# Earlier loads, spread stores and edge transposes on VectorE in a graph-network kernel

## The chip, the cores and the metric

The kernel runs on one core of one Trainium2 chip. The metric is the device time of one execution in microseconds (us). The kernel before takes 17,993.09 us, the median of three runs (17,978.58 to 18,013.7).

## The reference

There are 50,000 nodes with a row x of 160 numbers each (64 scalars and 32 vectors of 3), and 1,650,000 directed edges (src, dst), sorted by dst, with four numbers `edge_attr_4` each. Every node also has one edge to itself among them. Cut to what matters:

```python
ss, vv = s[src], v[src]                       # gather the source's row
out0 = C0 * (ss * e0 @ W1 + dot * INV3 @ W2)  # linear in x[src], and in the edge's four numbers
...
m_agg = jax.ops.segment_sum(m, dst, num_segments=n)
hs = m_agg[:, :MUL0] @ Ws * LIN_S
hv = jnp.einsum('nui,uw->nwi', m_agg[:, MUL0:].reshape(n, MUL1, 3), Wv) * LIN_V
x = _layernorm(x + (x + jax.nn.relu(h)))
```

A message is linear in x[src] and in the edge's four numbers. So for each node it is enough to sum four weighted copies of the gathered rows (one for each number k) and to multiply the sums by one combined matrix afterwards. The kernel does that.

## The kernel before

**Units, groups, pairs, stages.** A unit is 128 edges. A group is G = 6 units (768 edges); the kernel has 2087 groups and 12,522 units. A pair is two groups (12 units), 1044 in all; a stage is 20 groups, that is ten pairs, 105 stages. The program is written out in full, in one long loop over the pairs (the loop at the end of the function, `for p, (s, g, ng) in enumerate(pairs)`).

**One pair.** `gather` (L344 on) issues 12 indirect DMAs on POOL (L349), each of which fetches 128 rows of x into a slice of the tile `xg`; the pool of `xg` has four buffers, so the gathers of a pair wait until TensorE has read those of four pairs earlier. `spread` (L353 on) makes on VectorE a one-hot tile `hot` (L358) that says which of 32 node slots an edge belongs to, and `ha` (L361), the one-hot times each of the four edge numbers. `group_sums` (L386) multiplies on TensorE: `ha` of a unit stands as the weights, the gathered rows are the moving data, and six units add up in PSUM. `turn_sums` transposes the result in 32x32 blocks on VectorE (L398) and adds it (L405) at a place known only at run time to `ring`, a tile that holds the sums of a segment of 512 nodes (four blocks of 128). When a new segment begins, the tail of the old ring is added to the head of the new one (L402).

**One stage.** `load` asks on the SP queue for the indices and numbers of the next stage (L257 from the list `edges`, or L263 to L265 from the inputs for the first five stages), at the stage's first pair. `place`, four pairs later, brings them from one unit on a partition to one edge of each unit on a partition: TensorE transposes source and target indices (L326, L327) and the four numbers (L331) into PSUM, and a matmul with ones (L320) spreads the first node of each group, taken out by VectorE (L318), to all partitions; VectorE then makes `baseB` (L322), the integer indices `si` (L334) for the gathers, and `rel` (L337). In TensorE's queue these matmuls stand between those of L386, and TensorE runs its queue in order.

**Packs.** A node's edge to itself needs no gather. For all but the first 100 groups these edges are taken out: a pack is 128 rows of 790 edges. `read` fetches them on SP (L474 to L478, a tile of one buffer); ScalarE and VectorE mark the edges to themselves, move the others together by log-steps of predicated copies (L566), sum the four numbers of the ones taken out, and `store` writes each row by a DMA of its own to a place known at run time in `edges`, and its self-numbers to `selves` (L618, 16 DMAs a step after a read of registers, L601). There are 16 packs. A pack is a list of 77 steps, 17 of them stores, which are dealt out evenly between the end of the last pack and the pack's due pair.

**Blocks.** When a block of 128 nodes is complete, `block` multiplies its columns of the ring by the combined weights (L704), VectorE adds the node's own rows `xt` (asked for by L644 at the pair at which the block's last group runs) and norms them (L182 to L196), ScalarE takes the root (L191), SP writes two blocks (L784). For the edges to themselves, `ask_own` (six pairs before the segment) fetches 256 rows of x four times, once to each 32 partitions, in one DMA (`xr`, L675), and one number for each row (`sr`, L676: 1024 pieces of four bytes); `set_own` (two pairs before) multiplies them on VectorE (L689) and transposes them into the new ring (L693), which they start.

**What orders the work.** On SP, TensorE, VectorE and ScalarE the instructions run in the order in which the program writes them; `after_pair(p, f)` puts a task in a list that is handed over when pair p is written, and `work(1.0)` writes one unit of such tasks after each of the 12 units of a pair. SP's queue holds all loads and stores, and a DMA that must wait for its data (L784 for VectorE's `o`) holds those behind it.

Of the kernel before, what the change touches and what calls it, by code (L numbers as in the profile page):

```python
# [50 lines left out]
P = 128  # L51
MUL0, MUL1 = 64, 32
D = MUL0 + 3 * MUL1
NK = 4
# [21 lines left out]
KM = 31  # L76

# [25 lines left out]
def tile_gnn_resnorm(ctx: ExitStack, tc: tile.TileContext, x, src, dst, attr, W1, W2, W3, W4, W5, Ws, Wv, out, n_edges):  # L103
# [123 lines left out]
    with tc.tile_pool(name="once", bufs=1) as once, tc.tile_pool(name="raw", bufs=2) as rawp, \  # L227
# [17 lines left out]
        nc.vector.tensor_copy(slotsP, slots)  # L245

# [3 lines left out]
        def load(s):  # L250

            g0 = s * SG
            n = (min(NG, g0 + SG) - g0) * G
            if g0 >= NH:
                p0 = g0 * G * P - EH
                r6 = rawp.tile([P, P, 2 + NK], F32, name="r6")
                dq.dma_start(r6[:n].rearrange("u p c -> u (p c)"),  # L257
                             edges[0, p0 * (2 + NK):(p0 + n * P) * (2 + NK)].rearrange("(u q) -> u q", u=n))
                return s, n, None, r6[:n, :, 0], r6[:n, :, 1], r6[:n, :, 2:]
            e = slice(g0 * G * P, (g0 * G + n) * P)  # L260
            ri = rawp.tile([P, 2, P], I32, name="ri")
            ra = rawp.tile([P, P, NK], F32, name="ra")
            dq.dma_start(ri[:n, 0, :], src1[e].rearrange("(u p) o -> u (p o)", p=P))  # L263
            dq.dma_start(ri[:n, 1, :], dst1[e].rearrange("(u p) o -> u (p o)", p=P))
            dq.dma_start(ra[:n].rearrange("u p k -> u (p k)"), attr[e].rearrange("(u p) k -> u (p k)", p=P))  # L265
            return s, n, ri, None, None, ra[:n]

        def cast(loaded):
            s, n, ri, sf, df, af = loaded
            if ri is not None:  # L270
                rf = rawp.tile([P, 2, P], F32, name="rf")
                begun.append(nc.scalar.copy(rf[:n], ri[:n]))
                sf, df = rf[:n, 0, :], rf[:n, 1, :]
            return s, n, sf, df, af
# [37 lines left out]
        def place(cast_):  # L312

            s, n, sf, df, af = cast_
            ng = n // G

            first = idxp.tile([P, SG], F32, name="first")
            nc.vector.tensor_scalar(first[:n], starts[:n], df[:, 0:1], None, op0=ALU.mult)  # L318
            yield 1
            nc.tensor.matmul(bank[:, 3, :ng], ones[:n], first[:n, :ng], start=True, stop=True)  # L320
            baseB = idxp.tile([P, SG], F32, name="baseB")
            nc.vector.tensor_scalar(baseB[:, :ng], bank[:, 3, :ng], float(N - 1), None, op0=ALU.min)  # L322
            aim(s, ng, baseB)
            yield 1
            pi = bank[:, 1:3, :]
            nc.tensor.transpose(pi[:, 0, :n], sf, ident[:n, :n])  # L326
            nc.tensor.transpose(pi[:, 1, :n], df, ident[:n, :n])  # L327
            yield 1.5
            pk = psK.tile([P, NK, P], F32, name="pk")
            for k in range(NK):  # L330
                begun.append(nc.tensor.transpose(pk[:, k, :n], af[:, :, k], ident[:n, :n]))  # L331
                yield 0.75
            si = idxp.tile([P, P], I32, name="si")
            nc.vector.tensor_scalar(si[:, :n], pi[:, 0, :n], 0.0, float(N - 1), op0=ALU.max, op1=ALU.min)  # L334
# [3 lines left out]
                rel[:, :n].rearrange("p (g j) -> p g j", j=G), pi[:, 1, :n].rearrange("p (g j) -> p g j", j=G),  # L338
                float(N - 1), baseB[:, :ng].unsqueeze(2).to_broadcast([P, ng, G]),
# [3 lines left out]
            placed[s] = si, rel, pk  # L343
# [50 lines left out]
        def turn_sums(p, ps):  # L394
# [4 lines left out]
            for i in range(ng):  # L399
                k = seg_of[g + i]  # L400
                if k and g + i == first_of[k]:
                    nc.vector.tensor_tensor(ring[k][:, :, :TW - S], ring[k][:, :, :TW - S], ring[k - 1][:, :, S:],  # L402
                                            op=ALU.add)
# [337 lines left out]
        def after_pair(p, f, *args):  # L741
            later.setdefault(p, []).append((f, args))
# [313 lines left out]
```

## Time and profile before

| what | value |
|---|---|
| median of three runs | 17,993.09 us |
| time of the profiled execution | 18,022.17 us |
| its span | 18,020.0 us |
| busy: POOL, VectorE, TensorE matmul, ScalarE | 12,137.8, 7,032.6, 6,879.0, 227.8 us |
| DMA engines' mean share | 24% on POOL's queue, 6% on SP's |
| granted TensorE clock | 0.625 |

The profile's page has the busy time of each engine, the span in 40 slices, DMA queues, the chain that ended last, and groups of instructions with what ended the idle time before them. Asked further, the trace gives waits by engine and line, and the instructions of a stretch in order of time. "Issue" is idle time that ends with nothing that the trace shows; "remote" is a semaphore that something outside the traced instructions raised, or one that the trace could not assign.

### The profile page before, as it was taken

How to read it: one execution, taken by the hardware profiler on the slowest of the kernel's cores; microseconds unless marked ns; L12 is line 12 of the kernel's file. 1: busy time of each engine (PE TensorE's matmuls, PEld its weight loads, DVE VectorE, ACT ScalarE, POOL GpSimd, SP SyncE). 2: the span in 40 equal slices, each digit the busy share in tenths (PEclk: the TensorE clock that was granted, in tenths of full speed). 3: DMA queues.
4: the chain of work that ended last, by engine and by line, in shares of the span. 5: the costliest groups of instructions: out<-in, count | busy, mean ns of one | idle time of the engine just before them, and what ended most of it. 6: DMA issues, size and time to landing. Idle time of an engine off the chain costs nothing. (4 is left out here: it accounts for less than half of the span.)

```text
span 18020.0 us, 99721 instructions
## 1 busy us (share of the span) xinstructions
PE 6879.0 (38%) x29811; PEld 6014.7 (33%) x29812; DVE 7032.6 (39%) x11269; ACT 227.8 (1%) x479; POOL 12137.8 (67%) x12535
## 2 busy tenths in 40 slices
PE   3333334343333333333333333334333333333333
PEld 3333333333333333333333333333333333333333
DVE  4343443434434343443433434344343433434332
ACT  0000000000000000000000000000000000000000
POOL 6666666666666666666666666666666666666666
PEclk6666666666666666666666666666666666666666
DMA  2222323232232322323223232322323223232222
GB/s 71 74 69 72 80 71 81 69 82 72 73 79 70 83 71 73 79 69 81 72 72 79 70 79 72 82 69 72 80 70 82 69 73 80 69 79 72 73 72 63
DMA packets 961715, 1337.18 MB, mean 74 GB/s; under 512 B 411739, under 2 KB 716048, under 8 KB 957182
## 3 DMA queue, kind: packets, MB, share of 16 engines
q0 software_dynamic: 601056, 1026.60, 23.7%
q1 hardware_dynamic: 358674, 302.87, 6.1%
q8 instruction: 238, 3.90, 0.1%
q14 instruction: 307, 2.51, 0.0%
q10 hardware_dynamic: 1440, 1.29, 0.0%
HBM read 1258.50 MB, written 71.40 MB: 74 GB/s over the span
## 5 line engine op out<-in xcount | busy, mean ns | idle before, releaser
L349 POOL DMA_INDIRECT xg<-in_x,si x12522 | 12134.1, 969 | 5859.5 <-issue 3666.1
L386 PE MATMUL ps<-xg,ha 128*128 128x160 f32 x25044 | 6255.4, 383 | 9081.8 <-issue 8146.9
L386 PEld LDWEIGHTS ps<-xg,ha 128*128 128x128 f32 x25044 | 5171.1, 254 | 9859.0 <-issue 8902.6
L398 DVE STREAM_TRANSPOSE sums<-ps 128x320 f32<-128x320 f32 x1044 | 529.7, 507 | 6341.5 <-remote 4050.5
L361 DVE TENSOR_TENSOR ha<-hot,pk 128x1536 f32<-128x1536 f32 x1044 | 1830.2, 1753 | 35.8
L182 DVE SCALAR_TENSOR_TENSOR y<-phb,xt 128x160 f32<-128x160 f32 x391 | 125.6, 321 | 3508.3 <-PE ps L386 1623.2
L704 PE MATMUL phb<-BWk,ring 128*128 128x160 f32 (+1 forms) x3910 | 1181.7, 388 | 454.0 <-issue 452.9
L704 PEld LDWEIGHTS phb<-BWk,ring 128*128 128x128 f32 (+1 forms) x3910 | 925.6, 266 | 470.0 <-issue 469.5
L405 DVE TENSOR_TENSOR ring<-ring,sums 128x160 f32 x2087 | 683.1, 327 | 309.7 <-issue 224.2
L358 DVE TENSOR_TENSOR hot<-bank,rel 128x384 f32<-128x384 f32 x1044 | 572.4, 548 | 107.0 <-remote 70.5
L693 DVE STREAM_TRANSPOSE ring<-xr 128x1280 f32<-128x1280 f32 x188 | 466.1, 2479 | 6.5
L566 DVE COPY_PREDICATED prow<-marks,prow 128x2370 f32<-128x2370 int32 (+8 forms) x160 | 445.4, 2784 | 1.1
L320 PE MATMUL bank<-first,ones 120*128 120x20 f32 (+1 forms) x210 | 59.4, 365 | 815.1 <-DVE first L318 573.0
L320 PEld LDWEIGHTS bank<-first,ones 120*128 120x128 f32 (+1 forms) x210 | 49.8, 292 | 853.6 <-DVE first L318 597.5
L191 ACT ACTIVATE rstd<-mv,eps_t 128x1 f32<-128x1 f32 x391 | 115.2, 295 | 17061.4 <-DVE st L184 5415.1
L326 PE MATMUL bank<-ident,r 120*128 120x120 f32 x100 | 46.2, 462 | 703.1 <-issue 361.0
L566 DVE COPY_PREDICATED pra<-marks,pra 128x1580 f32<-128x1580 int32 (+8 forms) x160 | 306.5, 1915 | 0.0
L689 DVE TENSOR_TENSOR xr<-xr,sr 128x1280 f32<-128x1280 f32 x188 | 277.0, 1473 | 57.4 <-DMA sr<-selves 35.9
L326 PEld LDWEIGHTS bank<-ident,r 120*128 120x128 f32 x100 | 21.1, 211 | 727.4 <-issue 369.7
L196 DVE TENSOR_SCALAR o<-y,mv,rstd 128x160 f32<-128x160 f32 x391 | 146.1, 374 | 19.6 <-issue 3.7
L402 DVE TENSOR_TENSOR ring<-ring 128x1280 f32<-128x1280 f32 x97 | 143.0, 1474 | 1.8
L331 PE MATMUL pk<-ident,r 120*128 120x120 f32 (+1 forms) x400 | 139.5, 400 | 0.0
(349 smaller groups left out, 2156.2 us busy)
## 6 DMA issues: line engine op xcount, KB each, us to landing
xg<-in_x,si POOLq DMA_INDIRECT x12522
xr<-in_x SPq DMA_DIRECT2D x187, 640.0 KB
edges<-prow SPq DMA_DIRECT2D x1994, 18.5 KB
r<-edges SPq DMA_DIRECT2D x99, 360.0 KB
selves<-mine SPq DMA_DIRECT2D x1992, 0.5 KB
xt<-in_x SPq DMA_DIRECT2D x195, 160.0 KB
out<-o SPq DMA_DIRECT2D x195, 160.0 KB
pra<-in_attr SPq DMA_DIRECT2D x15, 1580.0 KB
```

Of the source, the lines that this page charges most:

```text
L196: nc.vector.tensor_scalar(o[:n], y[:n], mv[:n, 0:1], rstd[:n], op0=ALU.subtract, op1=ALU.mult)
L349: nc.gpsimd.indirect_dma_start(out=xg[:, j, :], out_offset=None, in_=x, in_offset=bass.IndirectOffsetOnAxis(ap=placed[0][:, u + j:u + j + ...
L358: nc.vector.tensor_tensor(hot[:, :n], slotsP[:, 0:W].unsqueeze(1).to_broadcast([P, n, W]), rel[:, u:u + n].unsqueeze(2).to_broadcast([P, n ...
L361: nc.vector.tensor_tensor(ha[:, :n], hot[:, :n].unsqueeze(2).to_broadcast([P, n, NK, W]), pk[:, :, u:u + n].rearrange("p k u -> p u k").un ...
L386: mm = nc.tensor.matmul(ps[:, j // G, :], ha[:, j].rearrange("p k w -> p (k w)"), xr, start=j % G == 0, stop=j % G == G - 1)
L398: nc.vector.transpose(at[:, :ng], ps[:, :ng].rearrange("p g (b f) -> p g b f", f=FB))
L402: nc.vector.tensor_tensor(ring[k][:, :, :TW - S], ring[k][:, :, :TW - S], ring[k - 1][:, :, S:], op=ALU.add)
L405: nc.vector.tensor_tensor(here, here, at[:, i], op=ALU.add)
L566: nc.vector.copy_predicated(what[:n, a:e], mi[:, r].unsqueeze(2).to_broadcast([n, e - a, what.shape[2]]), what[:n, a + d:e + d])
L689: nc.vector.tensor_tensor(xr[:, :nq], xr[:, :nq], sr[:, :nq].unsqueeze(2).to_broadcast([P, nq, D]), op=ALU.mult)
L693: nc.vector.transpose(ring[k][:, :, c0:c0 + nq * W].rearrange("p b (w q) -> p q b w", q=nq), xr[:, :nq].rearrange("p q (b f) -> p q b f", ...
L704: wrote("misc", nc.tensor.matmul(ph[:nb], ring[k][:, i, c0:c0 + nb], BWk[:, i, :], start=i == 0, stop=i == ND - 1))
```

## The change

1. **Loads.** `load` is asked for three pairs earlier (`LEAD = 3`), and it fetches in another layout: a partition gets four runs of 32 edges, one from each of four units. It always fetches 128 units. The first node of each group comes by a small DMA of its own (L269, `fi` or `fd`).
2. **Turning.** `place` uses VectorE's 32x32 transpose three times (L343, L349, L352) in place of the matmul with ones and the six transposes on TensorE.
3. **Packs.** The reading of the next pack (`follow`) stands in front of the last pack's stores; the stores come in every other step, and 15 empty steps follow. With these a pack is 105 steps (the first 109), and the due pair is earlier, by three pairs or two.
4. **Own rows.** `xr` comes in four DMAs (L700) in four successive pairs, from eight pairs before the segment; `selves` comes as it lies (`sa`, L705: 128 pieces of 128 bytes), and VectorE picks the number: `sa` times a mask in PSUM (L711), a sum (L712) into PSUM, and `xr` times that (L713).
5. **Rings.** The tail of the old ring is added in five instructions of some 133 to 166 columns (L425) in place of one of 1280.
6. **Node rows.** `xt` is asked for three pairs earlier.

The lines of the changed kernel are those of its own listing. Cut to its core:

```diff
+REST = 15
+LEAD = 3
+        shareP, sumP = bank[:, 3, 64:64 + NK], bank[:, 3, 96:96 + BP * P // W]
@@ load
-                r6 = rawp.tile([P, P, 2 + NK], F32, name="r6")
-                dq.dma_start(r6[:n].rearrange("u p c -> u (p c)"),
-                             edges[0, p0 * (2 + NK):(p0 + n * P) * (2 + NK)].rearrange("(u q) -> u q", u=n))
+            def fetch(to, what, c):
+                rows = what.rearrange("(u i q) -> i u q", u=P, i=NK)
+                dq.dma_start(to, rows)
+            def fetch_first(to, what, c):
+                firsts = what.rearrange("(g q) -> g q", g=W)[:, 0:1]
...
+                    dq.dma_start(to, firsts.unsqueeze(0).to_broadcast([NK, W, 1]))
...
+                r6 = rawp.tile([P, NK, W, C], F32, name="r6")
+                fd = rawp.tile([P, 1], F32, name="fd")
+                fetch_first(fd, edges[0, q0 * C + 1:(q0 + W * G * P) * C + 1], C)
+                fetch(r6.rearrange("p b e c -> p b (e c)"), edges[0, p0 * C:(p0 + P * P) * C], C)
@@ place
-            nc.vector.tensor_scalar(first[:n], starts[:n], df[:, 0:1], None, op0=ALU.mult)
-            yield 1
-            nc.tensor.matmul(bank[:, 3, :ng], ones[:n], first[:n, :ng], start=True, stop=True)
-            nc.vector.tensor_scalar(baseB[:, :ng], bank[:, 3, :ng], float(N - 1), None, op0=ALU.min)
+            nc.vector.transpose(baseB, fd.to_broadcast([P, W]))
+            base = baseB[:, f0:f0 + ng]
+            nc.vector.tensor_scalar(base, base, float(N - 1), None, op0=ALU.min)
...
-            nc.tensor.transpose(pi[:, 0, :n], sf, ident[:n, :n])
-            nc.tensor.transpose(pi[:, 1, :n], df, ident[:n, :n])
-            yield 1.5
+            nc.vector.transpose(pi.rearrange("p c (l b) -> p c b l", b=NK), ef)
+            yield 1
             pk = psK.tile([P, NK, P], F32, name="pk")
-            for k in range(NK):
-                begun.append(nc.tensor.transpose(pk[:, k, :n], af[:, :, k], ident[:n, :n]))
-                yield 0.75
+            begun.append(nc.vector.transpose(pk.rearrange("p k (l b) -> p k b l", b=NK), af.rearrange("p b e k -> p k b e")))
+            yield 1
@@ turn_sums
-                    nc.vector.tensor_tensor(ring[k][:, :, :TW - S], ring[k][:, :, :TW - S], ring[k - 1][:, :, S:],
-                                            op=ALU.add)
+                    past = max(high[first_of[k - 1]:first_of[k]]) + W - k * S
+                    for b in range(ND):
+                        nc.vector.tensor_tensor(ring[k][:, b, :past], ring[k][:, b, :past], ring[k - 1][:, b, S:S + past],
+                                                op=ALU.add)
@@ pack
-            steps += [read, None, None, None, begin]
+            steps.append(begin)
...
-            steps += [None, None]
-            steps += [None, None]
+            steps += [None, None, follow, None]
...
-                steps.append(partial(store, head, j))
-            return steps + [stored]
+                steps += [partial(store, head, j), None]
+            return read, steps + [stored] + [None] * REST
@@ set_own
-            xr, sr, nq = got
-            nc.vector.tensor_tensor(xr[:, :nq], xr[:, :nq], sr[:, :nq].unsqueeze(2).to_broadcast([P, nq, D]), op=ALU.mult)
+            xr, sa, nq = got
+            nc.vector.tensor_tensor(sa[:, :nq], sa[:, :nq], shareP.unsqueeze(1).to_broadcast([P, nq, NK]), op=ALU.mult)
+            nc.vector.tensor_reduce(sumP[:, :nq], sa[:, :nq], axis=AX.X, op=ALU.add)
+            nc.vector.tensor_tensor(xr[:, :nq], xr[:, :nq], sumP[:, :nq].unsqueeze(2).to_broadcast([P, nq, D]), op=ALU.mult)
@@ the plan and the loop over pairs
-            due.append(min((first - 1) * per - 1, first_of[own] // PG - 7))
-            packs.append(pack(i))
+            due.append(min((first - 1) * per - 1 - LEAD, first_of[own] // PG - 9))
+            packs.append(pack(i, lambda i=i: reads[i + 1]() if i + 1 < npacks else None))
+        packs[0][:0] = [reads[0], None, None, None]
...
-                after_pair(p - 6, ask_own, k, bs, got)
+                for part in range(NK):
+                    after_pair(p - 8 + part, ask_own, k, bs, got, part)
...
-            after_pair(max(p, START - 1), do_ahead, b)
+            after_pair(max(p - 3, START - 1), do_ahead, b)
...
+            if (p + LEAD) % per == 0 and (p + LEAD) // per + 1 < NSC or not p:
+                ahead_ = (p + LEAD) // per + 1
...
+                raws[ahead_] = load(ahead_)
             if p % per == 0 and s + 1 < NSC:
-                raws[s + 1] = load(s + 1)
```

## Prediction

> **What bounds the kernel now.** I read the page's busy shares and groups first, then POOL's waits, then stretches of the timeline.
>
> ```profile
> span 18020.0 us, 99721 instructions
> PE 6879.0 (38%) x29811; PEld 6014.7 (33%) x29812; DVE 7032.6 (39%) x11269; ACT 227.8 (1%) x479; POOL 12137.8 (67%) x12535
> ...
> L349 POOL DMA_INDIRECT xg<-in_x,si x12522 | 12134.1, 969 | 5859.5 <-issue 3666.1
> ```
>
> POOL's gathers fill the span. One takes 949 ns in the median (the tile view of xg), and 0.306 us lie behind each (3666.1 / 11991 below), so 12,522 of them need 15,715 us. What lies above that is of two kinds: long gathers, 12,134.1 - 12,522 x 0.949 = 251 us, and stands.
>
> ```profile
> POOL xg L349 <- issue: 3666.1, 11991, 2.1
> POOL xg L349 <- PE ps L386: 1224.7, 236, 46.9
> POOL xg L349 <- remote: 875.2, 223, 7.0
> POOL xg L349 <- PE phb L704: 64.3, 12, 6.7
> ```
>
> With two single waits of 5.9 and 5.6 the stands are 2,176 us in 473 pieces, 4.6 us each, nearly all ahead of a pair's first gather: xg has four buffers, and TensorE has not yet read the pair four back. TensorE and VectorE are 38% and 39% busy, so it is waiting and not work that makes them late. A stretch shows how:
>
> ```profile
> 3023.17 1.75 DVE L361 TENSOR_TENSOR ha<-hot,pk 128x1536 f32<-128x1536 f32 x1
> 3054.79 0.32 DVE L182 SCALAR_TENSOR_TENSOR y<-phb,xt 128x160 f32<-128x160 f32 x1 [29.87 <-remote]
> ```
>
> ```profile
> 3006.24 0.95 POOL L349 DMA_INDIRECT xg<-in_x,si  x1 [6.21 <-PE phb L704]
> 3057.40 0.94 POOL L349 DMA_INDIRECT xg<-in_x,si  x1 [6.22 <-remote]
> ```
>
> POOL runs from 3006 to 3051. From 3026 on TensorE's instructions come 0.7 or 1.4 us apart though nothing shown holds them, VectorE waits 30 us for a semaphore of TensorE's, and only 3.6 us after POOL has stopped does it come. Of VectorE's waits over 6 us for sums (L398) and y (L182), 7,618 of 9,188 us end inside a stand. So the loop catches up while POOL stands, and then runs on for two or three pairs. This pattern fills stages with and without stores alike (168 to 178 us each, with few exceptions). No part of the change aims at it, and I leave most of it in place.
>
> **The change part by part,** against the profiled execution's 18,022.17 us (29 above the median).
>
> (1) *Long gathers.* This is the surest part.
>
> ```profile
> 3064.53 1.48 DVE L689 TENSOR_TENSOR xr<-xr,sr 128x1280 f32<-128x1280 f32 x1
> 3064.92 1.91 POOL L349 DMA_INDIRECT xg<-in_x,si  x1 [0.30 <-issue]
> ...
> 3068.38 2.31 POOL L349 DMA_INDIRECT xg<-in_x,si  x1 [0.30 <-issue]
> 3068.40 1.47 DVE L689 TENSOR_TENSOR xr<-xr,sr 128x1280 f32<-128x1280 f32 x1
> ```
>
> The gather beside the product L689, which reads two SBUF tiles, takes 1 to 1.4 us more. Over the trace, 132 gathers over 1.1 us lie mostly beside L689 (160 us over 0.96 each), 81 beside L402 (47 us), 46 beside L693 (17 us), 22 elsewhere. VectorE's ha (L361, 1.75 us, one operand in PSUM) has none. In the change the second operand of L689's successor lies in PSUM, so its 160 us should go. L402 becomes five instructions of some 155 columns; L405, with 160 columns and two SBUF operands, has 2 long gathers among 2,087, so I take the 47 us off too: 207 us. Not all of it reaches the end: a POOL that runs faster meets the full buffers earlier. Over the stages, one us more of long gathers goes with 0.54 us less of stands (a weak link, correlation -0.12). So 207 x 0.46 = 95 to 207; I take 150. The Trainium skill (SBUF — State Buffer, Who interferes with whom) says that a VectorE instruction with two SBUF inputs and a GpSimd instruction that reads SBUF hold each other up; by it alone L425's five pieces would still block and only the 160 would go.
>
> (2) *SP's queue.* Four stands are out of proportion: 46.9 us at pair 45, 20.9 at 484, 12.9 at 617, 19.6 at 937. At the first, second and last VectorE waits for xt (93.1 us at most), at the third for a pack's prow.
>
> ```profile
> DVE y L182 <- DMA xt<-in_x: 241.7, 7, 93.1
> ```
>
> xt's request stands in SP's queue behind stores. The first pack's 17 store steps went out between 530 and 809 us, 16.4 us each, while its 77 steps were dealt to 37 pairs of 17.2 us, 8.3 us each. After, 109 steps in some 34 pairs, stores in every second one: 10.7 us. The lag falls from 17 x 8.1 = 138 to 97 us, and xt is asked three pairs (51 us) earlier: about half of that stand remains. Other packs have some 65 pairs: 14.5 us a store step before, 21 after, above the 16.4 needed, so the rest goes. Excess over 4.6 us is 100.3 - 18.4 = 82; less half of the first (21), 60. Bounds: 0 and 82.
>
> (3) *Place off TensorE.*
>
> ```profile
> PE bank L320 <- DVE first L318: 573.0, 51, 39.2
> ...
> PE bank L326 <- issue: 405.7, 26, 52.8
> PE bank L326 <- DVE baseB L322: 339.3, 26, 25.6
> ```
>
> With the smaller rows (80.1, 69.1, 48.5) TensorE stands 1,516 us at these two lines, with the matmuls of L386 behind them; VectorE waits for TensorE's answers in turn, 267 us at L322, 107 each at L334 and L358, 481 in all. Some 287 us of TensorE's busy time go too (59.4, 46.2, 139.5, L327 like L326). Most of this is hidden. What shows is where the place falls: it is written in the sixth pair of a stage, whose xg the tenth pair waits for. Stands of the tenth pairs sum to 363 us; the other nine places have 200 on average, and the pair after it 115, 85 less. Net 77 to 162 us; bounds 0 and 481 (all of VectorE's waits); I take 100, near the rows of the tenth pairs.
>
> (4) *VectorE's additions.* The three transposes have 32, 256 and 512 columns; L398 takes 508 ns for 320, L693 2,485 for 1,280, so 1.59 to 1.94 ns a column: 0.15 + 0.45 + 0.90 = 1.5 us x 105 = 158. L711 and L712: at most L405's 327 and L341's 278 ns, I take 0.37 together x 188 = 70. L425: 5 x 0.32 for 1.474, +13. L318 goes, -22. Sum 219, on an engine that idles 6,341 us ahead of L398. I charge POOL's standing share, 12%: 26 us; bounds 0 and 219. The skill (VectorE: DVE Perf Modes, Rules for kernel authors) prefers TensorE for a 128x128 transpose into PSUM, and so speaks against this part; six at L331's 400 ns are 2.4 us on an engine that is just as idle, so by work alone the part would be near nothing, and its gain is the handing to and fro.
>
> (5) *Nothing charged:* 187 x 1024 four-byte pieces go, SP's 12 to 15 us holds at the second xr go, loads come in 512 pieces of 768 bytes (3,072 bytes took 121 ns, 640 took 32, so 4 x 38 against 121) and 331 more SP rows are written. Three to seven pairs of lead (51 to 120 us) cover them; without cover a late load holds VectorE in place and TensorE behind it.
>
> Sum: 150 + 60 + 100 - 26 = 284. 18,022 - 284 = 17,738; less 29, **17,710**.
>
> **Rivals.**
> - *A: stands take it back.* POOL's saved time turns into stands and place's gain into VectorE's work; (2) alone remains: 17,993 - 60 = 17,930. For it: 7,618 us of waits that end only in stands. Against: long gathers are not followed by fewer stands one for one.
> - *B: no change,* the store lag stays too: 17,993 within 36.
> - *C: slower.* VectorE runs in order and now waits itself for the loads and does 219 us more, all in series between a sum's arrival and the next ha; with (1) at its lower end, 17,993 + 219 - 95 = 18,117. With no more than those 95 us gained, it decides from 131 of the 219 us on the path (60%). Against: 6.1 us idle a pair at L398, against 0.21 added.
> - *D: the chain loosens.* All 481 us of waits come off, with 207 and 82: 17,993 - 770 + 26 = 17,250.
> - That the stores are not thinned out: the written order has each store step still as one run of 16 DMAs, so only the steps lie further apart; that is in (2).
>
> **How the numbers follow.** 0.2% (36 us) is about what a measurement here can tell from no change. Forecast (17,580 to 17,860) 0.52; A (to 17,957) 0.17; B 0.10; C 0.12; D and what lies towards it (under 17,580) 0.09. Faster 0.78, same 0.10, slower 0.12. The range reaches from 17,480, with part of D, to 18,030, with A and B: about 0.2 is left out.
>
> **What would show it.** (1) POOL's busy time near 11,930 us and gathers beside L713 at 0.95 us; (2) no wait of y for xt over 20 us but one near 800 us; (3) tenth pairs' stands like the others'; (4) VectorE's busy time near 7,250 us. Wrong, if the stands (2,176 us) grow by more than 100 us, or if L349 waits long for si.

## The result and the profile after

The changed kernel takes 17,886.03 us (median of four runs, 17,883.85 to 17,893.28) against 17,992.18 of the kernel before beside it: a ratio of 0.9941, 95% interval 0.9929 to 0.9953, 106 us less. The forecast was 284 us less. The profiled execution took 17,885.21 us, 137 less than the profiled one of before.

The head of the page after, and POOL's row among the groups (busy us, mean ns of one, idle time before it):

```profile
span 17883.5 us, 99696 instructions
## 1 busy us (share of the span) xinstructions
PE 7054.6 (39%) x28971; PEld 6119.6 (34%) x28972; DVE 7272.7 (41%) x12244; ACT 226.7 (1%) x484; POOL 11914.2 (67%) x12535
...
L370 POOL DMA_INDIRECT xg<-in_x,si x12522 | 11910.4, 951 | 5949.2 <-issue 3663.3
```

POOL is busy 223.6 us less (12,137.8 before) and VectorE 240 us more. So far this is what the prediction asked for. POOL's waits after (total us, times, longest):

```profile
POOL xg L370 <- issue: 3663.3, 11955, 2.0
POOL xg L370 <- PE ps L407: 1417.8, 283, 8.1
POOL xg L370 <- remote: 781.0, 192, 6.7
POOL xg L370 <- PE phb L728: 52.2, 9, 7.0
```

The four stands of 12.9 to 46.9 us are gone; apart from one of 9.4 at the start none is longer than 8.1. Yet the rows of stands sum to 2,251 (before 2,164). Counted gather by gather (idle over 1 us before a gather), the stands are 2,165 us before and 2,261 after: +96, with 424 and 460 pieces. Take the 82 us of outsized stands out of before and the ordinary ones have grown by some 180 us, beside 222 us of long gathers that went (257 us over 0.96 us a gather before, 35 after). The net is 224 less busy, 96 more standing, 7 less of the short gaps: 135 of the 137.

The parts did on their engines what they should. First POOL's gathers in the tile view of xg (ns: shortest, median, longest), then the own rows' product among the groups of the page:

```profile
L370 POOL DMA_INDIRECT xg<-in_x,si x12522: 942/949/3261, 11.8 to 17863.0; - x199
```

```profile
L713 DVE TENSOR_TENSOR xr<-xr,bank 128x1280 f32<-128x1280 f32 x188 | 278.8, 1483 | 6.7 <-issue 0.4
```

L713 takes the 1.48 us that L689 took, but no gather beside it is long now: 28 gathers take over 1.1 us, of 281 before. The queue's sign is there too: VectorE's waits for xt (241.7 us, longest 93.1) have gone from the list altogether.

One stretch of the timeline after shows what is still there (start, duration, engine, operation, idle before it):

```profile
9033.82 0.43 PE L407 MATMUL ps<-xg,ha 128*128 128x160 f32 x1 [2.38 <-issue]
...
9036.62 0.43 PE L407 MATMUL ps<-xg,ha 128*128 128x160 f32 x1 [2.37 <-issue]
...
9042.42 0.95 POOL L370 DMA_INDIRECT xg<-in_x,si  x1 [0.30 <-issue]
...
9049.24 2.22 PE L407 MATMUL ps<-xg,ha 128*128 128x160 f32 x7 [0.29 <-issue]
9049.33 0.33 DVE L184 SCALAR_TENSOR_TENSOR y<-phb,xt 128x160 f32<-128x160 f32 x1 [24.61 <-PE ps L407]
...
9049.87 0.94 POOL L370 DMA_INDIRECT xg<-in_x,si  x1 [6.50 <-PE ps L407]
```

As before, TensorE's instructions come 1.4 us apart (two records 2.8 apart, one of weights between) while POOL gathers, and VectorE waits 24.61 us. POOL stops at 9043.4; six us later TensorE runs seven matmuls in 2.2 us, and VectorE and POOL go on.

### The profile page after: what moved, and what is told of

Read it like the earlier page. It is cut to its first block, busy times and chain, and to the rows that moved or that the text cites. A ratio compares the mean times of both kernels' runs of the same rounds, so it can differ in the third digit from the quotient of the medians.

```text
span 17883.5 us, 99696 instructions
## 1 busy us (share of the span) xinstructions
PE 7054.6 (39%) x28971; PEld 6119.6 (34%) x28972; DVE 7272.7 (41%) x12244; ACT 226.7 (1%) x484; POOL 11914.2 (67%) x12535
## 5 line engine op out<-in xcount | busy, mean ns | idle before, releaser
L370 POOL DMA_INDIRECT xg<-in_x,si x12522 | 11910.4, 951 | 5949.2 <-issue 3663.3
L407 PE MATMUL ps<-xg,ha 128*128 128x160 f32 x25044 | 6513.3, 393 | 10316.0 <-issue 9211.1
L407 PEld LDWEIGHTS ps<-xg,ha 128*128 128x128 f32 x25044 | 5393.7, 262 | 11235.4 <-issue 10130.0
L713 DVE TENSOR_TENSOR xr<-xr,bank 128x1280 f32<-128x1280 f32 x188 | 278.8, 1483 | 6.7 <-issue 0.4
L425 DVE TENSOR_TENSOR ring<-ring 128x196 f32<-128x196 f32 (+20 forms) x485 | 149.3, 373 | 1.8
L186 DVE BATCH_NORM_STATS2 st<-y 128x6 f32<-128x160 f32 x391 | 128.1, 328 | 13.4
L675 DVE MEMSET ring<- 128x1280 f32 (+1 forms) x98 | 119.3, 1218 | 22.9 <-issue 22.9
L586 DVE COPY_PREDICATED_SCALAR hit<-marks,none 128x395 int32 (+8 forms) x160 | 105.1, 657 | 5.7
L352 DVE STREAM_TRANSPOSE pk<-r 128x512 f32<-128x512 f32 x100 | 104.6, 1046 | 0.0
L587 DVE COPY_PREDICATED hit<-marks,pri 128x395 int32<-128x395 int32 (+8 forms) x160 | 95.7, 598 | 6.2 <-DVE hit L586 0.7
```

Source lines behind the costliest of these rows:

```text
L370: nc.gpsimd.indirect_dma_start(out=xg[:, j, :], out_offset=None, in_=x, in_offset=bass.IndirectOffsetOnAxis(ap=placed[0][:, u + j:u + j + ...
L407: mm = nc.tensor.matmul(ps[:, j // G, :], ha[:, j].rearrange("p k w -> p (k w)"), xr, start=j % G == 0, stop=j % G == G - 1)
L425: nc.vector.tensor_tensor(ring[k][:, b, :past], ring[k][:, b, :past], ring[k - 1][:, b, S:S + past], op=ALU.add)
L713: nc.vector.tensor_tensor(xr[:, :nq], xr[:, :nq], sumP[:, :nq].unsqueeze(2).to_broadcast([P, nq, D]), op=ALU.mult)
```

## The experiments

The sums in the tables are counted from each trace: "stands" is idle time over 1 us before a gather, "holds" is what gathers take over 0.96 us. Ratios are to the kernel before, run beside each kernel on the same chip, with 95% intervals. The chips differ: before takes 17,998 us on one, 18,003 on a second and 18,136 to 18,144 on a third, so times are compared as ratios, or between kernels that ran side by side. The only trace of the kernel before is the one shown with the prediction, of 18,022.17 us.

| kernel | ratio | 95% interval | POOL's gathers | stands (pieces) | holds | stands + holds |
|---|---|---|---|---|---|---|
| before (its profile) | 1 | | 12,134 | 2,165 (424) | 257 | 2,422 |
| changed | 0.9941 | 0.9929–0.9953 | 11,910 | 2,261 (460) | 35 | 2,296 |
| p1_port | 1.0020 | 1.0010–1.0030 | 11,878 | 2,571 (482) | 36 | 2,606 |
| p3_queue | 0.9977 | 0.9968–0.9986 | 12,103 | 2,275 (444) | 258 | 2,533 |
| p13_port_queue | 0.9981 | 0.9972–0.9990 | 11,878 | 2,525 (476) | 36 | 2,561 |
| e_pause | 1.0829 | 1.0812–1.0845 | 11,876 | 2,241 (448) | 34 | 2,275 |
| c_after (changed again) | 0.9943 | 0.9928–0.9958 | 11,876 | 2,302 (456) | 35 | 2,337 |
| e_bufs5 | 0.9984 | 0.9975–0.9993 | 11,877 | 2,378 (460) | 36 | 2,414 |
| e_half | 0.9890 | 0.9875–0.9905 | 11,902 | 2,163 (376) | 35 | 2,198 |
| e_narrow | 0.9948 | 0.9933–0.9963 | 11,881 | 2,299 (447) | 40 | 2,338 |
| e_lock | 0.9937 | 0.9923–0.9950 | 12,043 | 2,114 (424) | 199 | 2,313 |
| e_hold | 0.9944 | 0.9928–0.9959 | 12,821 | 1,302 (217) | 963 | 2,264 |
| e_twice | 0.9944 | 0.9928–0.9959 | 11,875 | 2,306 (478) | 34 | 2,340 |
| e_ahead | 0.9936 | 0.9923–0.9950 | 11,876 | 2,279 (421) | 35 | 2,314 |
| e_single | 0.9927 | 0.9912–0.9943 | 11,872 | 2,468 (665) | 32 | 2,500 |
| e_ps3 | 0.9919 | 0.9906–0.9933 | 11,881 | 2,402 (464) | 39 | 2,440 |
| e_hold3 | 1.0118 | 1.0103–1.0134 | 13,976 | 555 (93) | 2,087 | 2,642 |
| e_late | 0.9923 | 0.9909–0.9936 | 11,868 | 2,424 (475) | 28 | 2,452 |
| c_after2 (changed again) | 0.9924 | 0.9910–0.9938 | 11,877 | 2,409 (482) | 35 | 2,444 |
| p13_again | 0.9981 | 0.9972–0.9990 | 11,877 | 2,522 (482) | 35 | 2,558 |

Rows p1_port to e_pause and e_single to p13_again ran where before takes 18,136 to 18,144 us, c_after to e_narrow where it takes 17,998, e_lock to e_ahead where it takes 18,003.

My first theory for the missing 150 us was G: what POOL saves on its own, it stands later. The rival was V: VectorE's 219 us of added work, in the loop from TensorE's sums to the next ha, ate the gain. A third, S, came from G: the number of buffers of xg counts the stands.

**p1_port: the port part alone, on the kernel before.**

```diff
+        sumP = bank[:, 3, 96:96 + BP * P // W]
@@ set_own
-            nc.vector.tensor_tensor(xr[:, :nq], xr[:, :nq], sr[:, :nq]...
+            nc.vector.tensor_copy(sumP[:, :nq], sr[:, :nq])
+            nc.vector.tensor_tensor(xr[:, :nq], xr[:, :nq], sumP[:, :nq]...
@@ turn_sums: the ring's tail in five instructions, as in the change
```

> The kernel before with two parts of the change alone: the product's second operand (L689) copied into PSUM first, and the ring's tail added in five narrow instructions. Long gathers should fall from 251 us to under 50 in every theory. Theory G (the loop of TensorE and VectorE sets the pace while gathers run, and POOL's stands are what is left over): the stands grow by about as much, time 17,990 to 17,940. Rival V (the gain is real and VectorE's added work in place and set_own ate it): the 207 us come off here, where that work is not added, 17,790 to 17,850.

The ratio was 1.0020 (1.0010 to 1.0030), 32 us slower. The holds went from 257 to 36 us, as in the whole change, and the kernel was no faster, with hardly any work added to VectorE. V doesn't explain that. What POOL no longer spends in gathers is not missing from the time, so it went into standing (2,571 us here).

**p3_queue and p13_port_queue: the queue part alone, and both.** The queue part is the change's loads three pairs ahead in the old layout, `follow`, a store in every second step with the 15 empty ones, xt three pairs earlier, and xr in four DMAs in four pairs.

```diff
@@ pack
-            steps += [None, None]
-            steps += [None, None]
+            steps += [None, None, follow, None]
...
-                steps.append(partial(store, head, j))
+                steps += [partial(store, head, j), None]
-            return steps + [stored]
+            return read, steps + [stored] + [None] * REST
@@ the loop over pairs
-            after_pair(max(p, START - 1), do_ahead, b)
+            after_pair(max(p - 3, START - 1), do_ahead, b)
```

> The kernel before with SP's parts alone: loads three pairs earlier in the old layout, next pack read before the last stores, stores in every other step, xt three pairs earlier, xr in four DMAs; turning stays on TensorE, L689 as it was. The three stands for xt and the one for prow (100 us together) go. Both theories: 17,890 to 17,940; G adds that nothing else in the stands moves, so that this part is nearly the whole of the change's 106 us.

> Both together: the whole change but for the turning on VectorE and sa. G: 17,870 to 17,930, the same as the change within 0.3%. V: 17,700 to 17,760, faster than the change by 150 us, since VectorE's 240 us are not added.

The heads of the two pages, p3_queue first:

```profile
span 18086.4 us, 100462 instructions
PE 6905.6 (38%) x29811; PEld 6033.5 (33%) x29812; DVE 7031.1 (39%) x11269; ACT 226.2 (1%) x479; POOL 12106.4 (67%) x12535
```

```profile
span 18113.3 us, 101066 instructions
PE 7075.1 (39%) x29811; PEld 6176.8 (34%) x29812; DVE 7074.1 (39%) x11845; ACT 226.1 (1%) x479; POOL 11882.1 (66%) x12535
```

The queue alone gives 0.9977, that is 0.23% or 42 us of 18,136; with the port part 0.9981. So the port part adds nothing on this base either: side by side on one chip its holds are 222 us less, its stands 250 us more. G had put p13_port_queue within 0.3% of the whole change, and V 150 us ahead of it; at 0.9981 it is 0.6% behind (0.9924 on this chip, below), so both missed. What the whole change has beyond these two is the turning on VectorE, with the loads in the layout for it and the own rows' numbers picked from `sa`.

**e_pause: POOL's own time, added.** In the changed kernel two iotas of 128x790 (POOL instructions that fill a tile with counted numbers, which nothing reads) stand in the middle of each pair's gathers.

```diff
@@ gather
             for j in range(n):
+                for _ in range(2 if j == 6 else 0):
+                    nc.gpsimd.iota(idle, pattern=[[1, L]], base=1, ...)
                 nc.gpsimd.indirect_dma_start(
```

> The changed kernel with two iotas of 128x790 (0.79 us each in the profile) added to POOL in the middle of each pair: 1044 x 1.6 = 1,670 us more busy time on POOL. G: the stands (2,284 us) shrink by most of it, time within 2% of the change (under 18,250). If POOL's own time sets the pace and stands come on top at random: 17,886 + 1,670 = 19,550.

```profile
span 19628.5 us, 101782 instructions
PE 7308.6 (37%) x28971; PEld 6215.8 (32%) x28972; DVE 7278.4 (37%) x12244; ACT 226.4 (1%) x484; POOL 13542.2 (69%) x14621
```

In the head of its page POOL is busy 13,542.2 us, 1,662 more than in c_after2 (11,880 with its other work), and the ratio is 1.0829 where the changed kernel has 0.9924 on such a chip: 0.0905 x 18,136 = 1,641 us. The iotas came in full, the stands stayed (2,241). So G as I had put it is false: time in which POOL works on something else than gathers, at this place, does not shorten its stands. Standing comes on top of such work.

**c_after, e_bufs5, e_half, e_narrow: what the stands are counted by.** c_after is the changed kernel as a control. The others change it in one point each.

```diff
@@ e_bufs5 (room for it from the pool of hot and ha)
-            tc.tile_pool(name="rows", bufs=4) as rowp,  tc.tile_pool(name="ops", bufs=3) as op,
+            tc.tile_pool(name="rows", bufs=5) as rowp,  tc.tile_pool(name="ops", bufs=2) as op,
@@ e_half, group_sums
+                if j % 2:
+                    yield ps
+                    continue
@@ e_narrow, gather
-                    out=xg[:, j, :], out_offset=None, in_=x,
+                    out=xg[:, j, 0:16], out_offset=None, in_=x.rearrange("n (t f) -> (n t) f", f=16),
```

> The changed kernel itself once more, beside the next three, so that they are compared on one chip. Ratio to the kernel before 0.993 to 0.995; stands of POOL 2,250 to 2,450 us in some 460 pieces.

> The changed kernel with five buffers of xg in place of four, and two of ha and hot in place of three to make room. The longer pause experiment has shown that stands do not shrink when POOL is given more of its own work. Theory S (TensorE's and VectorE's chain gets stuck while gathers run and is freed only by a stand of about 4.7 us, so the stands are counted by the pairs that the buffers hold): one stand to 3.3 pairs in place of 2.3, about 310 x 4.7 = 1,460 us, time some 800 us shorter than the changed kernel. Rival L (the chain has a rate of its own, slower than POOL's, and buffers only delay): the same time within 0.3%.

> The changed kernel with the matmuls of every second unit left out (half of the edges are gathered but not summed). If the chain is stuck because TensorE's own instructions come slowly beside gathers (0.7 or 1.4 us apart, 48 to a pair): half of them, the stands fall under 1,000 us, time 16,200 to 17,000. If what sticks is the handing over from TensorE to VectorE, whose number stays: stands above 1,800 us, time over 17,400.

> The changed kernel with gathers of 16 columns in place of 160 (64 bytes a row, of other rows of x, repeated to 160 columns on TensorE's side; the sums are of other data). POOL's own time should stay at 0.95 us a gather. If the bytes or the DMA engines hold the chain up, stands fall under 1,000 us (16,200 to 17,000); if the issuing of gathers on POOL does, they stay above 1,800 us and the time within 2%.

A fifth buffer of xg does not help: 0.9984, 0.4% slower than the control (L had it within 0.3%), stands 2,378, still one every two or three pairs; TensorE only falls further behind the gathers (51 us in the median, 34 in the control, from a pair's last gather to its last matmul). S falls, with the reserve that the room came from hot and ha, which have one buffer fewer. Half of the matmuls gone takes TensorE's busy time from some 7,050 to 4,004 us, but the stands only from 2,302 to 2,163: TensorE's amount of work is not it. Rows of 64 bytes in place of 640 change nothing (2,299), though POOL's DMA queue then takes 7.0% of the DMA engines' time in place of 23.7%, so neither bytes nor the DMA engines' load is it.

**e_lock, e_hold, e_twice: is a hold as good as a stand?** After G had fallen one reading was left, H: when VectorE holds POOL in a gather, that does for the loop what a stand does. e_lock undoes the port part in the changed kernel; e_hold adds holds; e_twice adds the same work on VectorE without a hold.

```diff
@@ e_lock
-            nc.vector.tensor_reduce(sumP[:, :nq], sa...
+            sumS = ownp.tile([P, BP * P // W], F32, name="sumS")
+            nc.vector.tensor_reduce(sumS[:, :nq], sa...
...
-                    for b in range(ND):
-                        nc.vector.tensor_tensor(ring[k][:, b, :past], ...
+                    nc.vector.tensor_tensor(ring[k][:, :, :TW - S], ring[k][:, :, :TW - S], ring[k - 1][:, :, S:], op=ALU.add)
@@ e_hold, spread, ahead of ha's own instruction
+            nc.vector.tensor_tensor(ha[:, :n], hot[:, :n]..., rel[:, u:u + n]..., op=ALU.mult)
@@ e_twice, at the same place
+            nc.vector.tensor_tensor(ha[:, :n], hot[:, :n]..., pk[:, :, u:u + n]..., op=ALU.mult)
```

> The changed kernel with its port part alone undone: the product of the own rows reads both operands from SBUF again, and the ring's tail is added in one instruction. Theory H (a hold of POOL by VectorE frees the loop as a stand does, so the long gathers that went came back as stands): POOL's time over 0.96 us a gather rises from 35 to 230 to 260 us, the stands fall by about as much (2,302 in the control to 2,050 to 2,150), most of it in the two pairs after the product, and the time stays within 0.2% of the changed kernel (ratio to the kernel before 0.992 to 0.997). Theory P (the long gathers were a real cost, 150 us or more, and something else ate the gain): the stands stay at 2,300 and the ratio goes to 1.002 or more.

> The changed kernel with one more instruction of VectorE in each pair, of the size of ha's (128x1536) and with both operands in SBUF (its result is written over by ha). It holds up the gather beside it by 1.2 to 1.6 us in each of 1,044 pairs, 1,250 to 1,700 us in all. To be read against e_twice, which adds the same work without the hold. H: the holds do the work of stands, so the stands fall by 1,000 us or more (to under 1,300) and the time lies within 300 us of e_twice. T (held time adds in full, as the added iotas did): the stands stay at 2,100 to 2,400 and the time lies 1,250 us or more above e_twice.

> The changed kernel with ha's instruction (128x1536, one operand in PSUM) given twice in each pair: 1.75 us of VectorE a pair, 1,830 us in all, no hold of POOL. Theory V (VectorE's work lies on the path at each stand): every stand comes that much later, 452 stands x 1.75 to 3.5 us, ratio 1.035 or more. If VectorE's work is hidden behind the 17 us of a pair's gathers: within 0.5% of the changed kernel. POOL's standing share of 12% gives 220 us, ratio 1.007.

The head of e_hold's page and its POOL waits, and after them the same of e_twice:

```profile
PE 7323.1 (41%) x28971; PEld 6100.6 (34%) x28972; DVE 9082.3 (51%) x13288; ACT 226.5 (1%) x484; POOL 12824.4 (72%) x12535
```

```profile
POOL xg L370 <- PE ps L409: 653.0, 198, 10.4
POOL xg L370 <- remote: 631.5, 130, 11.1
```

```profile
PE 7102.5 (40%) x28971; PEld 6288.3 (35%) x28972; DVE 9091.9 (51%) x13288; ACT 226.7 (1%) x484; POOL 11878.6 (66%) x12535
```

```profile
POOL xg L370 <- PE ps L410: 1281.5, 270, 13.0
POOL xg L370 <- remote: 868.9, 234, 7.0
```

This is the clearest result of the case. VectorE is equally busy in both (9,082 and 9,092 us). In e_hold POOL is busy 946 us more, and stands 1,004 us less (1,302 against 2,306), in 217 pieces against 478. The times are 17,900.79 and 17,900.11 us. e_lock says the same in the other direction: with the long gathers back (199 us, of 230 to 260 expected, against 35 in e_ahead and in the control) the stands are 2,114, where e_ahead, which ran beside it, has 2,279 and the control, on another chip, 2,302. The time is 17,888.88 us, a ratio of 0.9937, not above the changed kernel's. In the two pairs after a product the stands are 203 us less than the control's, in the pair itself 98 more. H holds, P falls: a long gather beside a VectorE instruction costs nothing here, up to e_hold's 963 us, since it takes the place of as much standing. V falls too: 1,830 us more on VectorE cost 0.1% or less (17,900 us beside 17,889 for e_lock and 17,885 for e_ahead, run side by side). The hold itself is as large as expected in kind, smaller in size (0.9 us an instruction, not 1.2 to 1.6).

The Trainium skill (SBUF — State Buffer, Who interferes with whom) states that a VectorE instruction with two SBUF inputs contends with a GpSimd instruction that reads SBUF, and one with at most one such input, outside the 2-port modes, does not. e_hold and e_twice agree: 963 us of holds against 34. For small instructions the trace after hardly shows it: L425's five pieces, of 133 to 256 columns (most have over 195, where the change speaks of 133 to 166 and the prediction of 155), have two SBUF inputs each, and beside its 485 instructions there were only 17 long gathers, 5.7 us in all.

**e_ahead, e_single, e_ps3, e_late: what the standing pays for.** With holds and stands exchangeable, it remained to find what needs the 2,300 us.

```diff
@@ e_ahead: hot and ha two pairs ahead
-                    has[p + 1] = spread(...)
+                    has[p + 2] = spread(...)
@@ e_single: twice as many hand-overs (xg in eight buffers, leads doubled in pairs, block's from two to three)
-PG = 2
+PG = 1
@@ e_ps3: a third buffer of ps
-            tc.tile_pool(name="psA", bufs=2, space=PSUM) as psA, tc.tile_pool(name="psM", bufs=2, space=PSUM) as psM,
+            tc.tile_pool(name="psA", bufs=3, space=PSUM) as psA, tc.tile_pool(name="psM", bufs=1, space=PSUM) as psM,
@@ e_late: y two pairs after the matmuls of phb
-            return norm1(np_, ph[:nb], xt[:nb], nb)
+            return ph, xt, nb
...
-            for d, f in ((2, do_block), (3, do_root), (4, do_store), (6, do_send)):
+            for d, f in ((2, do_block), (4, do_norm), (5, do_root), (6, do_store), (8, do_send)):
```

> The changed kernel with hot and ha made two pairs ahead in place of one (has[p + 2] in pair p; the pool of three holds them). TensorE then has the weights of one more pair in hand when VectorE is held at a late sum. If the loop TensorE to VectorE to TensorE by ha sets the stands: they fall by a third or more (2,302 to under 1,500), ratio 0.95 to 0.975, faster than the changed kernel. If a late hand-over of TensorE's semaphores sets them, whatever VectorE has ready: stands within 10%, ratio within 0.3% of the changed kernel.

> The changed kernel with pairs of one group in place of two (PG = 1; xg in eight buffers of half the size, all leads doubled in pairs so that they stay the same in time). Gathers and matmuls are the same in number; the hand-overs of sums from TensorE to VectorE and of ha back double, and the two ps buffers hold half as much. If the quiet time is paid per hand-over: stands go from 2,300 to 3,800 us or more, the ratio to the kernel before to 1.07 or more. If it is paid per gather or per time: stands stay at 2,100 to 2,500, ratio 0.99 to 1.01.

> The changed kernel with three PSUM buffers for ps in place of two (the bank is taken from the pool of phb, which keeps one). If the depth of ps sets how many pairs one stand frees: stands come every three to four pairs in place of every two to three and sum to 1,500 to 1,800 us, ratio 0.955 to 0.975. If their sum is fixed by something else: 2,200 to 2,400 us in fewer, longer pieces, ratio within 0.3% of the changed kernel.

> The changed kernel with y written two pairs after the matmuls of phb in place of at once (root, store and send two pairs later too). VectorE's 4,000 us of waits at y should go or move to sums. If these waits set the stands (sums and ha queued behind y): stands fall by 300 us or more, ratio under 0.98. If they only show a hand-over that is late anyway: the waits move to sums, the stands stay within 5%, ratio within 0.2% of the changed kernel.

None of them moved the time against the changed kernel on its kind of chip (0.9936 beside c_after's 0.9943, on the two chips that differ by 5 us; 0.9927, 0.9919 and 0.9923 beside c_after2's 0.9924). Twice as many hand-overs gave 665 stands in place of 482, but shorter ones, 2,468 us against 2,409. A third ps left them at one every two or three pairs. With y written later VectorE's waits moved from y to sums (in e_late's DVE waits):

```profile
DVE sums L419 <- remote: 5147.3, 307, 33.0
DVE sums L419 <- PE ps L407: 4311.9, 250, 35.8
```

and the stands stayed at 2,424. So the need is not paid per hand-over, not per buffer, and not by an order of VectorE's that could be loosened. No version beat the changed kernel measurably.

**e_hold3: can holds take the place of all stands?** The instruction of e_hold, three times a pair.

> The changed kernel with the added instruction of e_hold three times in each pair: 5.3 us more of VectorE and, at e_hold's 0.9 us each, some 2,800 us of holds, more than the 2,300 us of stands. If holds take the place of stands until none is left: stands under 500 us, and the time 300 to 800 us above the changed kernel (ratio 1.01 to 1.04), because the holds outgrow the need. If only the stands matter beyond some point, or VectorE's 12 us a pair now bind: stands stay over 1,000 us and the ratio goes over 1.05.

```profile
POOL xg L370 <- PE ps L413: 353.0, 267, 9.3
POOL xg L370 <- remote: 251.4, 54, 8.7
```

The holds are 2,087 us and the stands 555 in 93 pieces, one every ten or more pairs; the sum, 2,642, is 198 above the control's 2,444 and the ratio 1.0118 against 0.9924. So nearly all standing can be replaced, and beyond that the holds begin to cost. The stands did not quite fall under 500, and VectorE with 12,735 us busy may have its part in the 350 us; I did not separate the two.

**c_after2 and p13_again: the turning's own size,** on one chip.

> The changed kernel once more, as a control beside the next run on the same chip. Ratio to the kernel before 0.992 to 0.995, stands of 2,250 to 2,450 us.

> The kernel before with the port part and the queue part (p13_port_queue again), beside the changed kernel on the same chip; what lies between the two is the turning on VectorE with its loads and the own rows' numbers picked on VectorE. The forecast's 100 - 26 = 74 us for it would make this run 0.4% slower than the control. If the turning is worth nothing and the earlier difference lay between the chips: within 0.1% of the control. If it carries nearly the whole gain: 0.5% or more slower than the control, and the ratio to the kernel before within 0.2% of 1.

17,999.61 and 18,103.47 us: the turning with what belongs to it (the loads' layout, the own rows' numbers) gives 103.9 us, 0.58%; no run separates these. The stands by place in the stage: tenth pairs 518 us without it and 276 with it, first pairs 107 and 244, the other eight 1,897 and 1,889. In p3_queue, without the port part, the tenth pairs have 352.

**What the records of TensorE's semaphore add.** Of the 28,971 matmul records, 10,979 raise one and the same semaphore (the signal for which other engines wait) when they end, and the trace has the times of most of these raises (9,522 in the profile after, 8,879 in e_hold). I counted them in the stands of POOL and in all the rest of the time, in which it gathers, has the short gaps between gathers and, in e_pause, runs the iotas:

```
                     in stands, per us      in the rest, per us
before               3,921   1.81           5,586   0.35
after                4,244   1.88           5,278   0.34
e_pause              4,088   1.82           5,326   0.31
e_half               2,410   1.11           2,064   0.13
e_hold               2,098   1.61           6,781   0.41
e_hold3                848   1.53           7,692   0.43
```

In the profile after, 3,373 of the 4,191 intervals under 0.06 us lie in stands, an eighth of the time; they are 0.043 us in the median. In the rest of the time 1,695 of the 3,036 intervals from 0.5 to 3.6 us lie within 0.06 us of 0.7, 1.4, 2.1, 2.8 or 3.5 us, and 705 at 0.50 to 0.55. In the stretch shown above there is a raise at 9021.21, the next record is at 9049.31, and with it 12 come within 0.47 us, 5.9 us after POOL's last gather ended; at 9049.33 VectorE's y starts. Over the whole profile TensorE's matmuls start at 1.72 per us outside the stands and 0.92 in them, the other way round from the raises. So it is less TensorE's arithmetic that is late than the word of it: while POOL gathers the raises come out slowly (in stretches like this one TensorE's next instructions too), and in a stand the backlog comes out. POOL's iotas don't let it out: in e_pause's iotas with the gaps around them 365 raises come in 1,897 us, 0.19 per us. Nor is it in the hold itself that it comes out: in e_hold the rate is 0.46 per us in gathers over 1.3 us and 0.43 in the usual ones, so all gathers have more than the 0.38 of the profile after.

## Why the prediction was wrong

**The sign was right, so was the mechanism of (2), and that of (3) in part; the step that failed is in (1).** It is "207 x 0.46 = 95 to 207; I take 150": the long gathers were taken to lie on the path for at least 46% of their length, and they don't lie on it. POOL's time did fall by 224 us, the long gathers by 222. What reached the end was 0: p1_port 1.0020, p13_port_queue against p3_queue 0.9981 against 0.9977, e_lock 0.9937 against the changed kernel's 0.9941. Holds turn into stands about one for one, not at 0.54: 222 us less of holds and 250 more of stands from p3_queue to p13_port_queue, 929 more and 1,004 less from e_twice to e_hold. I had fitted that figure over stages and called the link weak (correlation -0.12); stands of a stage may vary for other reasons too, and such noise can hide a link that is one for one. And I had the bound wrong: "95 to 207" left out the zero that rival A gave as a case. What the sentence on POOL that "meets the full buffers earlier" said was right, only to the full amount.

**(2) SP's queue, 60 us:** measured 42 alone (p3_queue). The stand at pair 45 was to be halved, the others to go; all four went, and yet only half of their 82 us of excess reached the time.

**(3) and (4), the turning, 100 - 26 = 74 us:** measured 104 net, with the loads' layout and the own rows' numbers, which (5) had put at nothing. Between p13_again and c_after2 the reading of places holds: tenth pairs fell by 242 us (518 to 276), first pairs took back 137, 105 net in stands; (3) had put the net at 77 to 162. But the 518 are not the 363 that (3) read: p3_queue has 352, so with the port part 166 us more came to stand in the tenth pairs, and the turning took these off too. From the profile before to the profile after tenth pairs fell by 99 and first pairs rose by 96, so by places alone nothing is left there. That the size came near the forecast is therefore partly luck. The charge of 26 us for VectorE was too high: e_twice gives it eight times as much work for 0.1% or less. VectorE's busy time was 7,272.7 us for the 7,250 forecast. The Trainium skill (VectorE: DVE Perf Modes, Rules for kernel authors) prefers TensorE for transposes of 128x128 into PSUM. No run here tests that preference: the change needs no such transposes, since its loads come in a layout for which VectorE's 32x32 blocks do, and the 104 us are those of the whole.

With 0 for (1) and 42 and 104 for the rest, the sum is 146; on the chip on which the parts were measured the whole change gives 136 (18,135.55 to 17,999.61), in the first pair of runs 106. The 40 us that are missing there stay open.

**The rivals.** A had the right mechanism for (1) (the stands take it back) and the nearest time, but its other half, place's gain lost in VectorE's work, was wrong. C fell: the change is faster, and in e_twice VectorE's work is off the path at eight times the amount, though not in place and set_own, where the change adds it. D fell as well: its 17,250 us are 636 below the measured time, and TensorE off the place did not loosen the chain beyond the tenth pairs.

**The signs.** POOL 11,914 us for 11,930; L713's gathers normal; no long wait for xt; tenth pairs 264 us beside 222 for the others in the profile after (363 and 200 before). "Wrong, if the stands grow by more than 100 us": they grew by 96 here and 137 in c_after, at the edge of that condition, and it was the right one to watch.

**What stays open.** Why TensorE's raises come out so slowly while POOL gathers, and why holds take the place of stands while iotas do not, no run here settles; the runs show only that it is so. The iotas stood at one place, in the middle of a pair; a pause of POOL's where the holds fall, or a longer one, was not tried. Nor did I try fewer raises from TensorE for the same matmuls, or the gathers from another engine.

## What to carry to other kernels

Before a saving on the engine that fills the span is counted, ask whether its idle time is a need of its own: shorten that engine's work and lengthen it by the same kind of time, and see whether its stands move against it. Here stands and holds together stayed nearly fixed (2,264 to 2,340 us in the control and in e_narrow, e_lock, e_hold, e_twice and e_ahead, on two chips that differ by 5 us; e_half with 2,198 and e_bufs5 with 2,414 lie outside), so taking holds away gained nothing, while work taken out of the loop's late places (place in TensorE's queue) and queues (SP) did gain. And a weak correlation over noisy stages is no exchange rate: two kernels that differ in the one thing are.

## What the hardware showed that I had not expected

- TensorE's recorded semaphore raises come at 1.88 per us in POOL's stands, most of them 0.043 us apart, and at 0.34 per us in the rest of the time, there often 0.7 us or a multiple of it apart (1,695 of 4,841 intervals in the profile after).
- A gather lengthened by a VectorE instruction with two SBUF operands (0.9 us each in e_hold) served as standing time of POOL; two iotas of 0.8 us a pair did not.
- Two chips differ by 0.8% on the kernel before (17,997.9 and 18,135.55 us) and by 0.6% on the changed one, and for the latter the difference lies in the stands: c_after and c_after2 have POOL's gathers at 11,876 and 11,877 us, stands of 2,302 and 2,409, and medians of 17,895.59 and 17,999.61 us.
